# Layer 0 with fp32 sums beside the count table and 16 dense blocks, the last sweep's blocks in the sweeps' PSUM banks, and attention in four stages

## The chip, the core and the metric

The kernel runs on one core of a Trainium2 chip. Five engines work from queues of their own: PE (TensorE, the matrix multiplier), DVE (VectorE), ACT (ScalarE), POOL (GpSimd) and SP (SyncE). In this kernel POOL issues the indirect gathers, SP issues nearly all other loads and stores, and ACT a few. The metric is device time in microseconds. Before the change it is the median of three runs.

## What is computed

A graph of N = 12500 nodes and E = 200000 edges, sorted by target. Each node has D = 256 features. Three layers take the mean over the incoming edges; a residual and a layernorm follow; then one attention step with K = 4 heads of R = 16, a gradient step, and a second layernorm.

```python
def _sage_layer(x, src, dst, inv_deg, W_self, W_neigh, b):
    agg = jax.ops.segment_sum(x[src], dst, num_segments=N_NODES)
    mean = agg * inv_deg[:, None]
    return x @ W_self + mean @ W_neigh + b
h = relu(_sage_layer(x, ...W0)); h = relu(_sage_layer(h, ...W1)); h = _sage_layer(h, ...W2)
z = _layernorm(x + h)

ZU = jnp.einsum('nd,kdr->knr', z, U)
logits = (ZU[:, src] * ZU[:, dst]).sum(-1) / sqrt(R)
alpha = softmax of logits over the edges of each dst
agg = segment_sum(alpha[..., None] * ZU[:, src], dst)
Z_half = 0.5 * z + 0.5 * einsum('k,knr,kdr->nd', softmax(head_w), agg, U)
residual = Z_half - (Z_half @ Dmat.T) @ Dmat
out = _layernorm(z + relu(Z_half + 0.5 * (residual @ Dmat) - 0.05))
```

## The kernel before

The edges are cut into NG = 112 groups of 1792 edges (14 columns of 128), in the order of their targets. Two ways lead to the sums of a layer.

*Groups.* POOL gathers the source rows of a group with 14 indirect DMAs (L118) into a buffer xg. DVE builds a one-hot matrix oh of edge against node (L458). ACT rounds the rows to fp32r (hi, L799), and DVE takes the rest (lo, L801), so that two fast matmuls, one of hi and one of lo, give fp32 accuracy. In layer 0 these are two matmuls per column j (L808, L809), in layers 1 and 2 one of twice the width (L805). All columns of a group add into pA; a carry (L465) shifts in the sums of the group before. sage_post then transposes the node's own row and the mean through the PSUM bank pT (L344, L368) and multiplies both by the weights into the bank pO (L348, L371). In layer 2, sage_end makes a layernorm, and project (L379 to L389) makes the attention's inputs, again through pT. finish hands out the tiles to store.

*Dense blocks.* The last NDL[l] blocks of 128 nodes of a layer go another way. During layer 0, form() builds a table cnt_d of how often each source occurs for each target: DVE compares (L626), PE multiplies (L634, 1024 matmuls), ACT writes bytes (L637) into the window tile win. A sweep runs over all 98 blocks of source rows for 4 (layer 0) or 8 (layers 1 and 2) target blocks at once. Each step loads rows hz and counts c8, ACT widens the counts (L706), and PE does 4 or 8 matmuls (L712) into the banks px. The results go to aggT (L724), and end_block finishes each target block like a group (L344, L348, L685, L689, and project in layer 2). The blocks of one sweep are finished during the next sweep; those of the last sweep follow at the layer's end.

NDL is (20, 32, 32): layer 0 has 90 groups and 490 sweep steps; layers 1 and 2 have 76 groups and 392 steps each.

*The order.* A Python loop over the groups emits everything. After each group, due(l, g) says how many sweep steps must have been emitted, and built(g) how many pieces of the table; the table is spread over the groups up to GB = 84. The last sweep's blocks begin at group NGS - LAG - sg, one per group, so the sweeps are spread over the groups up to there (66 in layers 1 and 2). A scheduler then reorders each engine's instructions by priority, with waits for data and for buffers; after() ties two instructions to an order by hand, as with the gathers and with PE's sweep steps. Two xg buffers are made at the start and filled early with the first two groups; layers 1 and 2 use a third one, "more". The one pT and the one pO bank serve groups and blocks alike.

*Attention.* For each of 112 groups SP loads zn, zb and the edges' row numbers, POOL gathers 14 columns of zs (four buffers), DVE builds oh, ACT the transposed one-hot ohT (L892, L893). For each half of the group PE spreads the target rows over the edges into pD (L905); DVE and ACT multiply, sum, exponentiate and weight (L910 to L923). PE adds up into pA (L926), with a carry (L465) from the group before; attention_post divides, transposes (L402), multiplies by gu into pO (L406), adds (L408) and makes the layernorm, and the group is stored. All of a group is emitted before the next group.

Of the kernel before, what the change touches and what calls it, by code (L numbers as in the profile page):

```python
# [9 lines left out]
F32 = mybir.dt.float32  # L10
F32R = mybir.dt.float32r
# [11 lines left out]
P = 128  # L23
NB = 125
TE = 125
GT = 14
# [5 lines left out]
ND = 32  # L32
NDL = (20, 32, 32)
SG0, SG = 4, 8
# [5 lines left out]
CP = 4  # L40
LAG = 2
G0 = 2
SMAX = 240.0
# [4 lines left out]
def tile_gnn_resnorm(  # L48
# [341 lines left out]

    def attention_post(wk, ps, zz, acc, eps=1e-16, op=OP.add):

        n = zz.shape[0]
        den = wk.tile([n, K], F32, name="den")
        nc.vector.tensor_scalar(den, acc[:, KR:AW], eps, None, op0=op)
        nc.vector.reciprocal(den, den)
        ag = wk.tile([n, KR], F32, name="ag")
        nc.vector.tensor_mul(ag.rearrange("p (k r) -> p k r", r=R),  # L398
                             acc[:, :KR].rearrange("p (k r) -> p k r", r=R),
                             den.unsqueeze(2).to_broadcast([n, K, R]))  # L400
        pa = ps.tile([P, n], F32, name="pT")
        nc.tensor.transpose(pa[:KR], ag, ident[:n, :n])  # L402
        agT = wk.tile([KR, n], F32, name="agT")
        nc.scalar.activation(agT, pa[:KR], AF.Copy)
        pg = ps.tile([n, D], F32, name="pO")
        nc.tensor.matmul(pg, agT, gu, start=True, stop=True)  # L406
        g = wk.tile([n, D], F32, name="g")
        nc.vector.tensor_add(g, zz[:, D:], pg)  # L408
        nc.scalar.activation(g, g, AF.Relu, bias=shrink[:n])
        nc.vector.tensor_add(g, zz[:, :D], g)  # L410
        return g, layernorm(wk, g, g)

# [54 lines left out]
    def fast_sage():  # L467
        with ExitStack() as fx:
# [82 lines left out]
            def chained(first, last):  # L551
                if chain[0] is not None:
                    after(chain[0], first)
                chain[0] = last

            counted = [0]

# [49 lines left out]
            def form(pool, psum):  # L607
# [6 lines left out]
                for i, u in enumerate(parts):  # L614
# [3 lines left out]
                    for i0 in range(0, P, CP):  # L618
# [9 lines left out]
                        for c in range(CP):  # L628
                            d = (i0 + c) * NC % P
                            if d == 0:  # L630
                                win = pool.tile([P, NP], U8, name="win", bufs=2).rearrange(
                                    "p (b d) -> p b d", d=P)
# [11 lines left out]

            def finish(l, lk, hn, po):

# [7 lines left out]
                zu = lk.tile([P, KR], F32, name="zu")  # L654
                made = project(lk, ps, hn, zu)
                sq = lk.tile([P, KR], F32, name="sq")
# [3 lines left out]
                nc.vector.tensor_max(top, top, nrm)  # L660
                return [(zu, zu_d), (hn, z_d)], made

            def sweeps(l, dk, dps, lk):
# [8 lines left out]

                def end_block(k, d, aggT):
                    at = N0 + (k + d) * P
# [4 lines left out]
                    if l == L - 1:  # L679
                        xb = lk.tile([P, D], F32, name="xb")  # L680
                        nc.sync.dma_start(xb, x[rows, :])
                    _, _, po = sage_own(wk, ps, wts[l], hb, True)
                    pn = ps.tile([P, D], F32, name="pO")
                    for c in range(DC):
# [6 lines left out]
                    sage_end(lk, l, wts[l], pn, hn[:, :D], xb)  # L691
                    for t, to in finish(l, lk, hn, pn)[0]:
                        nc.sync.dma_start(to[rows, :], t)
# [32 lines left out]
                for block in left:  # L726
                    end_block(*block)
                    yield []
# [3 lines left out]
            BUILDS = 3 + NU * PER  # L732
            GA, G1, GB = 3, 7, 84

            def due(l, g):
                sg, ahead = (SG, 0) if l else (SG0, G1)
                n, end = NDL[l] // sg * NQ, cuts[NDL[l]].NGS - LAG - sg
                if g >= end:
                    return n + min(sg, g + 1 - end)
                return max(0, n * (g + 1 - ahead) // (end - ahead))  # L740

# [8 lines left out]
            for l in range(L):  # L750
# [6 lines left out]
                with ExitStack() as lx:  # L757
# [10 lines left out]
                    for g in range(cut.NGS):  # L768
# [5 lines left out]
                        load_rows([(hb, table), (xb, x)][:1 if xb is None else 2], *at)  # L774
                        oh = onehot(wk, nodes, srel, F32R)
                        ahead = l == 0 and g < G0
                        if ahead:
                            last = early[g][1]
                        k = turn % (G0 + 1 if l else G0)
                        turn += 1  # L780
                        if k < G0:
                            xg = early[k][0]
                        else:
                            xg = dk.tile([P, GT, XW], F32, name="more", bufs=1)
                        for j in range(0 if ahead else GT):
# [4 lines left out]
                        pa = ps.tile([P, 2 * D], F32, name="pA")  # L790

                        if l:
                            hl = dk.tile([P, GT, 2, D], F32R, name="hl", bufs=1)
                            hi, lo = hl[:, :, 0], hl[:, :, 1]
                        else:
                            hi, lo = (dk.tile([P, GT, XW], F32R, name=n, bufs=1) for n in ("hi", "lo"))
                        hf = hi.bitcast(F32)
                        for j in range(0, GT, 2):
                            nc.scalar.activation(hi[:, j:j + 2, :W], xg[:, j:j + 2, :W], AF.Copy)  # L799
                        for j in range(GT):  # L800
                            nc.vector.tensor_tensor(lo[:, j, :D], xg[:, j, :D], hf[:, j, :D], op=OP.subtract)  # L801
                        for j in range(GT):
                            stop = g == 0 and j == GT - 1
                            if l:
                                end = nc.tensor.matmul(pa, oh[:, j], hl[:, j].rearrange("p i d -> p (i d)"),  # L805
                                                       start=j == 0, stop=stop)
                            else:
                                nc.tensor.matmul(pa[:, :W], oh[:, j], hi[:, j, :W], start=j == 0, stop=False)  # L808
                                end = nc.tensor.matmul(pa[:, :D], oh[:, j], lo[:, j, :D], start=False, stop=stop)  # L809
                        if g:  # L810
# [60 lines left out]
    def fast_attention():  # L871
        loads[0] = None
        H = GT // 2
        with tc.tile_pool(name="att", bufs=2) as wk, \
                tc.tile_pool(name="att_c", bufs=1, space=PSUM) as cps, \
                tc.tile_pool(name="att_ps", bufs=1, space=PSUM) as ps:
            nodes = group_consts(cps)
            before = None
            for g in range(NG):
                zb = wk.tile([P, 2 * D], F32, name="zb", bufs=3)  # L880
                zn = wk.tile([P, KR], F32, name="zn", bufs=3)
# [5 lines left out]
                                  .to_broadcast([P, GT * P]))  # L887
                zs = wk.tile([P, GT, KR], F32, name="zs", bufs=4)
                for j in range(GT):
                    gather(zs[:, j], zu_d, srcI[:, g, j:j + 1])  # L890
                oh = onehot(wk, nodes, rel[:, g], F32R)
                nc.scalar.activation(ohT.rearrange("p j e -> p (j e)"), rT, AF.Abs, bias=npidx)  # L892
# [6 lines left out]

                w = wk.tile([P, GT, 2 * AW], F32R, name="w")  # L900
                for a in (0, H):

                    pd = ps.tile([P, (H + 1) * 2 * KR], F32, name="pD", bufs=2)
                    for j in range(H):
                        nc.tensor.matmul(pd[:, j * 2 * KR:(j + 1) * 2 * KR], ohT[:, a + j],  # L905
                                         z2.rearrange("p k i r -> p (k i r)"), start=True, stop=True)

# [14 lines left out]
                    nc.scalar.activation(w[:, a:a + H, :AW], wf, AF.Copy)  # L922
                    nc.vector.tensor_tensor(w[:, a:a + H, AW:], wf, w.bitcast(F32)[:, a:a + H, :AW], op=OP.subtract)  # L923
                pa = ps.tile([P, 2 * AW], F32, name="pA")
                for j in range(GT):
                    nc.tensor.matmul(pa, oh[:, j], w[:, j],  # L926
                                     start=j == 0, stop=g == 0 and j == GT - 1)
                if g:
                    carry(wk, pa[:, :AW], delta[:, g:g + 1], before)
                acc = wk.tile([P, AW], F32, name="acc")  # L930
                part = wk.tile([P, AW], F32, name="part")
                nc.scalar.activation(part, pa[:, AW:2 * AW], AF.Copy)
                nc.vector.tensor_add(acc, part, pa[:, :AW])
                before = acc
                o, made = attention_post(wk, ps, zb, acc, 1e-30, OP.max)
                store_rows([(o, out)], g, made)


# [100 lines left out]
    def general_attention():  # L1039
# [40 lines left out]
        with tc.tile_pool(name="go", bufs=1) as wk, tc.tile_pool(name="go_ps", bufs=1, space=PSUM) as ps:  # L1080
            with tc.For_i(0, NBLK, 1) as i:
                rows = ds(i * NB, NB)
                zb = wk.tile([NB, 2 * D], F32, name="zb")
                nc.sync.dma_start(zb, z_d[rows, :])
                ab = wk.tile([NB, AW], F32, name="ab")
                nc.sync.dma_start(ab, acc_d[rows, :])
                o, _ = attention_post(wk, ps, zb, ab)
                nc.sync.dma_start(out[rows, :], o)
# [42 lines left out]
```

## Time and profile before

| | |
|---|---|
| median of three runs | 9464.18 us (9428.15 to 9476.44) |
| the profiled execution | 9457.81 us, span 9455.6 us |
| PE busy in the span | 5646.7 us (60%), 23556 matmuls |
| DVE busy | 4240.9 us (45%) |
| ACT busy | 3917.2 us (41%) |
| POOL busy | 4898.6 us (52%), 4982 instructions |
| granted PE clock, mean | 0.73 |
| moved by DMA | 1392.21 MB, 147 GB/s |
| sweep matmuls L712 | 8232, 2511.0 us busy |
| gathers L118 in attention | 1568, 1503.9 us busy, 1375.3 us idle before them |

The span is counted from the first to the last instruction, and 2.2 us of the profiled execution lie outside it. The busy time of an engine is the sum of its instructions; the idle time before an instruction is put down to whatever it waited for last. "remote" means that the profile found no instruction that released it at that time.

### The profile page before, as it was taken

Reading aid. Unit: us, or ns where it says so; the run is one execution under the profiler, and the core shown is the slowest. Engines: PE = TensorE matmul, PEld = TensorE weight load, DVE = VectorE, ACT = ScalarE, POOL = GpSimd, SP = SyncE. Lnnn points to the kernel's source line nnn. Section 1 sums busy time; section 2 is a strip of 40 time slices with the busy share of each in tenths; the row PEclk is TensorE's granted clock in tenths of the full one; section 3 lists DMA queues with packets and bytes.
Section 4 is the critical chain, followed back from the end, with each engine's and each line's share of the span. In section 5 each row is a group of like instructions: output and inputs, shape, how many; then the busy total and the mean of one; then the engine's idle time right before and its main releaser. Section 6 shows DMA issues by size and latency. Waiting matters only on the chain. (4 is left out here: it accounts for less than half of the span.)

```text
span 9455.6 us, 88266 instructions
## 1 busy us (share of the span) xinstructions
PE 5646.7 (60%) x23556; PEld 4373.7 (46%) x23556; DVE 4240.9 (45%) x11180; ACT 3917.2 (41%) x7165; POOL 4898.6 (52%) x4982
## 2 busy tenths in 40 slices
PE   4666777676577777764778787775333333333333
PEld 2455555555455656553556565653223223332323
DVE  5756555555333333333334444444244444444444
ACT  3655555554344444432344444432233333333333
POOL 4565555555455555554454444443455555555554
PEclk7788888887788888887888888886555555555555
DMA  7665666665466565654555555542222222222222
GB/s 205 219 199 190 200 216 203 206 212 178 156 185 191 188 191 186 191 158 127 161 177 174 173 174 165 168 152 75 60 76 76 72 75 77 75 72 76 76 76 61
DMA packets 836883, 1392.21 MB, mean 147 GB/s; under 512 B 187554, under 2 KB 452282, under 8 KB 832271
## 3 DMA queue, kind: packets, MB, share of 16 engines
q1 hardware_dynamic: 590624, 834.82, 27.1%
q0 software_dynamic: 213312, 496.82, 18.6%
q10 hardware_dynamic: 32431, 54.80, 1.7%
q8 instruction: 189, 3.10, 0.1%
q14 instruction: 327, 2.68, 0.1%
HBM read 1175.63 MB, written 210.33 MB: 147 GB/s over the span
## 5 line engine op out<-in xcount | busy, mean ns | idle before, releaser
L712 PE MATMUL px<-c,hz 128*128 128x512 f32 x8232 | 2511.0, 444 | 53.3 <-issue 45.9
L118 POOL DMA_INDIRECT zs<-zu_d,srcI x1568 | 1503.9, 959 | 1375.3 <-DVE sh L464 700.2
L118 POOL DMA_INDIRECT xg<-h_d,srcI x1428 | 1384.2, 969 | 1167.5 <-issue 342.7
L712 PEld LDWEIGHTS px<-c,hz 128*128 128x128 f32 x8232 | 1643.3, 206 | 554.9 <-issue 225.1
L118 POOL DMA_INDIRECT xg<-in_x_dram,srcI x1232 | 1296.6, 1052 | 994.6 <-DVE lo L801 477.6
L706 ACT ACTIVATE c<-c 128x1024 fp32r<-128x1024 uint8 (+1 forms) x1274 | 1124.3, 897 | 1370.9 <-remote 502.9
L458 DVE TENSOR_TENSOR oh<-rel,gconst 128x1792 fp32r<-128x1792 f32 x354 | 712.1, 2012 | 1008.2 <-remote 591.9
L118 POOL DMA_INDIRECT more<-h_d,srcI x700 | 669.7, 957 | 930.3 <-issue 367.0
L348 PE MATMUL pO<-ws,hT 128*128 128x256 f32 x1304 | 459.8, 485 | 460.8 <-DVE hT L345 343.3
L637 ACT ACTIVATE win<-pc 128x392 uint8<-128x392 f32 x1024 | 477.0, 503 | 526.3 <-remote 275.0
L805 PE MATMUL pA<-hl,oh 128*128 128x512 f32 x2128 | 591.4, 421 | 65.3 <-issue 25.7
L402 PE MATMUL pT<-ident,ag 128*64 128x128 f32 x112 | 46.8, 418 | 907.2 <-DVE ag L398 886.9
L634 PE MATMUL pc<-ob,oa 128*128 128x392 bf16 x1024 | 350.3, 377 | 353.0 <-ACT win L637 187.0
L348 PEld LDWEIGHTS pO<-ws,hT 128*128 128x128 f32 x1304 | 288.4, 237 | 577.3 <-DVE hT L345 392.2
L371 PE MATMUL pO<-wn,hT 128*128 128x256 f32 x968 | 335.5, 481 | 365.5 <-DVE hT L369 279.4
L799 ACT ACTIVATE hl<-xg 128x512 fp32r<-128x512 f32 x714 | 406.0, 621 | 336.3 <-remote 173.4
L801 DVE TENSOR_TENSOR hl<-xg,hl 128x256 fp32r<-128x256 f32 x1428 | 518.7, 416 | 27.7 <-ACT hl L799 19.0
L406 PE MATMUL pO<-gu,agT 64*128 64x256 f32 x224 | 136.5, 711 | 622.3 <-issue 551.4
L805 PEld LDWEIGHTS pA<-hl,oh 128*128 128x128 f32 x2128 | 415.9, 197 | 175.9 <-issue 39.2
L926 PE MATMUL pA<-w,oh 128*128 128x136 f32 x1568 | 420.3, 427 | 123.4 <-DVE bn_rs L335 54.3
L801 DVE TENSOR_TENSOR lo<-xg,hi 128x256 fp32r<-128x256 f32 x1260 | 454.7, 415 | 84.2 <-ACT hi L799 50.6
L408 DVE TENSOR_TENSOR g<-zb,pO 128x256 f32<-128x256 f32 x112 | 47.1, 421 | 942.0 <-remote 727.5
(225 smaller groups left out, 9700.7 us busy)
## 6 DMA issues: line engine op xcount, KB each, us to landing
hz<-hs_d SPq DMA_DIRECT2D x637, 512.0 KB
c<-cnt_d SPq DMA_DIRECT2D x112, 896.0 KB
ohT<-rel_d SPq DMA_DIRECT2D x112, 896.0 KB
hs_d<-hs SPq DMA_DIRECT2D x218, 256.0 KB
cnt_d<-win ACTq DMA_DIRECT2D x32, 1568.0 KB
c<-cnt_d SPq DMA_DIRECT2D x70, 448.0 KB
zb<-z_d SPq DMA_DIRECT2D x112, 256.0 KB
h_d<-hn SPq DMA_DIRECT2D x218, 128.0 KB
```

The costliest lines, as they stand in the source:

```text
L118: return nc.gpsimd.indirect_dma_start(out=dst_ap, out_offset=None, in_=table, in_offset=bass.IndirectOffsetOnAxis(ap=idx, axis=0))
L348: nc.tensor.matmul(po, hT[:, 0, c], wts[0][:, c], start=c == 0, stop=alone and c == DC - 1)
L371: nc.tensor.matmul(po, hT[:, 1, c], wts[1][:, c], start=False, stop=c == DC - 1)
L458: nc.vector.tensor_tensor(oh, r.unsqueeze(2).to_broadcast([P, GT, P]), nodes.unsqueeze(1).to_broadcast([P, GT, P]), op=op)
L634: mm = nc.tensor.matmul(pc.rearrange("p b d -> p (b d)"), oa[:, c], ob[:, c], start=True, stop=True)
L637: nc.scalar.activation(win[:, :, d:d + NC], pc, AF.Copy)
L706: nc.scalar.activation(c32.rearrange("p (k d) -> p k d", d=P), c8[:, :, b % CB], AF.Copy)
L712: made.append(nc.tensor.matmul(px[f][i], hz[:, b % ZB, a:a + P].bitcast(F32R), c32[:, i * 512:(i + 1) * 512], start=b == 0 and part == 0, ...
L799: nc.scalar.activation(hi[:, j:j + 2, :W], xg[:, j:j + 2, :W], AF.Copy)
L801: nc.vector.tensor_tensor(lo[:, j, :D], xg[:, j, :D], hf[:, j, :D], op=OP.subtract)
L805: end = nc.tensor.matmul(pa, oh[:, j], hl[:, j].rearrange("p i d -> p (i d)"), start=j == 0, stop=stop)
L926: nc.tensor.matmul(pa, oh[:, j], w[:, j], start=j == 0, stop=g == 0 and j == GT - 1)
```

## The change

1. *Layer 0's blocks.* NDL[0] goes from 20 to 16: 94 groups, 392 sweep steps.
2. *Layer 0's sums.* Groups 0 to 62 (g <= GB) multiply the gathered rows xg by an fp32 one-hot, one fp32 matmul per column, without hi and lo. Later groups split as before, but hi and lo lie in the two win tiles, which the table no longer needs by then. GB goes from 84 to 62, so the table is built by then; due() spreads half of layer 0's steps up to GB and half after it.
3. *Buffers.* G0 goes from 2 to 3: three xg buffers from the start, in all layers, and "more" is gone.
4. *The last sweep's blocks.* They come two per group (`2 * (g + 1 - end)`), and LAG goes from 2 to 1, so the sweeps of layers 1 and 2 are spread over 71 groups. end_block and finish get an argument bank: these blocks use the px banks of the sweeps in place of pT and pO. Within a px pair i, `px0i` stands for pT and `px1i` for pO.
5. *Attention.* attention_post becomes three functions; a group is a generator with four stages. Per round the newest group's first stage is emitted, then the second stage of the group before, and so on. in_order ties PE's order: pD of the newest group, pA and carry of the one before, the transpose of the second before, pO of the third before. zs has six buffers instead of four, zb six instead of three, oh, w and acc three instead of two.

```diff
-NDL = (20, 32, 32)
+NDL = (16, 32, 32)
-LAG = 2
-G0 = 2
+LAG = 1
+G0 = 3
...
-    def attention_post(wk, ps, zz, acc, eps=1e-16, op=OP.add):
+    def attention_mean(wk, acc, eps, op):
...
+        return ag
+
+    def attention_turn(wk, ps, ag):
+        n = ag.shape[0]
         pa = ps.tile([P, n], F32, name="pT")
-        nc.tensor.transpose(pa[:KR], ag, ident[:n, :n])
+        turn = nc.tensor.transpose(pa[:KR], ag, ident[:n, :n])
         agT = wk.tile([KR, n], F32, name="agT")
         nc.scalar.activation(agT, pa[:KR], AF.Copy)
+        return agT, turn
+
+    def attention_end(wk, ps, zz, agT):
...
-        nc.tensor.matmul(pg, agT, gu, start=True, stop=True)
+        mm = nc.tensor.matmul(pg, agT, gu, start=True, stop=True)
...
-        return g, layernorm(wk, g, g)
+        return g, layernorm(wk, g, g), mm
...
+            WB = max(NP, GT * XW * 4)
...
-                                win = pool.tile([P, NP], U8, name="win", bufs=2).rearrange(
+                                win = pool.tile([P, WB], U8, name="win", bufs=2)[:, :NP].rearrange(
...
-            def finish(l, lk, hn, po):
+            def finish(l, lk, hn, po, bank=ps):
...
-                made = project(lk, ps, hn, zu)
+                made = project(lk, bank, hn, zu)
...
+            class Spare:
...
+                def tile(self, shape, dt, name):
+                    return self.pool.tile(shape, dt, name=f"px{('pT', 'pO').index(name)}{self.i}")
...
-                def end_block(k, d, aggT):
+                def end_block(k, d, aggT, bank=ps):
...
-                    _, _, po = sage_own(wk, ps, wts[l], hb, True)
-                    pn = ps.tile([P, D], F32, name="pO")
+                    _, _, po = sage_own(wk, bank, wts[l], hb, True)
+                    pn = bank.tile([P, D], F32, name="pO")
...
                 for block in left:
-                    end_block(*block)
+                    end_block(*block, Spare(dps, block[1] % (sc // 512)))
                     yield []
...
-            GA, G1, GB = 3, 7, 84
+            GA, G1, GB = 3, 7, 62
...
-                n, end = NDL[l] // sg * NQ, cuts[NDL[l]].NGS - LAG - sg
+                n, end = NDL[l] // sg * NQ, cuts[NDL[l]].NGS - LAG - sg // 2
                 if g >= end:
-                    return n + min(sg, g + 1 - end)
-                return max(0, n * (g + 1 - ahead) // (end - ahead))
+                    return n + min(sg, 2 * (g + 1 - end))
+                if l:
+                    return n * (g + 1) // end
+
+                return max(0, n * (g + 1 - G1) // (GB - G1) // 2 if g < GB else n - n * (end - g - 1) // (end - GB) // 2)
...
-                        oh = onehot(wk, nodes, srel, F32R)
+
+                        halved = l or g > GB
+                        oh = onehot(wk, nodes, srel, F32R if halved else F32)
...
-                        k = turn % (G0 + 1 if l else G0)
+                        xg = early[turn % G0][0]
...
-                            hi, lo = (dk.tile([P, GT, XW], F32R, name=n, bufs=1) for n in ("hi", "lo"))
+                        elif halved:
+                            hi, lo = (tk.tile([P, WB], U8, name="win", bufs=2).bitcast(F32R).rearrange(
+                                "p (j d) -> p j d", d=XW) for _ in range(2))
+                        if halved:
...
+                            first, stop = j == 0, g == 0 and j == GT - 1
...
+                            elif halved:
+                                nc.tensor.matmul(pa[:, :W], oh[:, j], hi[:, j, :W], start=first, stop=False)
+                                end = nc.tensor.matmul(pa[:, :D], oh[:, j], lo[:, j, :D], start=False, stop=stop)
                             else:
...
+                                end = nc.tensor.matmul(pa[:, :W], oh[:, j], xg[:, j, :W], start=first, stop=stop)
...
-            before = None
-            for g in range(NG):
-                zb = wk.tile([P, 2 * D], F32, name="zb", bufs=3)
+            order, sums = [None], [None]
+
+            def in_order(first, last):
+                if order[0] is not None:
+                    after(order[0], first)
+                order[0] = last
+
+            def group(g):
+
+                zb = wk.tile([P, 2 * D], F32, name="zb", bufs=6)
...
-                zs = wk.tile([P, GT, KR], F32, name="zs", bufs=4)
+                zs = wk.tile([P, GT, KR], F32, name="zs", bufs=6)
...
-                oh = onehot(wk, nodes, rel[:, g], F32R)
+                oh = onehot(wk, nodes, rel[:, g], F32R, bufs=3)
...
-                w = wk.tile([P, GT, 2 * AW], F32R, name="w")
+                w = wk.tile([P, GT, 2 * AW], F32R, name="w", bufs=3)
...
+                    in_order(mm[0], mm[-1])
...
+                yield
                 pa = ps.tile([P, 2 * AW], F32, name="pA")
...
+                    mm.append(carry(wk, pa[:, :AW], delta[:, g:g + 1], sums[0]))
+                in_order(mm[0], mm[-1])
...
-                before = acc
-                o, made = attention_post(wk, ps, zb, acc, 1e-30, OP.max)
+                sums[0] = acc
+                ag = attention_mean(wk, acc, 1e-30, OP.max)
+                yield
+                agT, mm = attention_turn(wk, ps, ag)
+                in_order(mm, mm)
+                yield
+                o, made, mm = attention_end(wk, ps, zb, agT)
+                in_order(mm, mm)
                 store_rows([(o, out)], g, made)
+
+
+            live = []
+            for g in range(NG + 3):
+                if g < NG:
+                    live.insert(0, group(g))
+                for s in list(live):
+                    if next(s, live) is live:
+                        live.remove(s)
```

## The prediction

> **What bounds the kernel now.** I read the busy time by stage first, then the timeline of one stretch of each stage, then the waits. The stages are cut where the gathers change table: 76 us is the first gather of layer 0's main loop, 2403 and 4381 the first of layers 1 and 2, 6705 the first of attention. Columns are microseconds and, in brackets, instructions.
>
> ```profile
> core 0: us, PE busy (x) PEld busy (x) DVE busy (x) ACT busy (x) POOL busy (x), PEclk, DMA share, GB/s
> 76.00:2403.00 2327.00, 1581.50 (x7533) 1169.87 (x7532) 1367.78 (x4419) 1228.88 (x2694) 1311.88 (x1248) 0.81 0.63 204
> 2403.00:4381.00 1978.00, 1402.83 (x5614) 1098.55 (x5614) 723.90 (x1730) 826.38 (x1340) 1024.88 (x1064) 0.84 0.57 178
> 4381.00:6705.00 2324.00, 1681.41 (x6663) 1281.38 (x6663) 933.37 (x2589) 852.02 (x1446) 1029.06 (x1064) 0.82 0.49 152
> 6705.00:9456.00 2751.00, 965.09 (x3694) 814.50 (x3694) 1185.40 (x2350) 1006.46 (x1678) 1503.93 (x1568) 0.50 0.26 74
> ```
>
> No engine is full in any stage. Attention is the emptiest: 2751/112 = 24.6 us a group, of which DVE works 10.6 and POOL's 14 gathers, 1.25 us from start to start, take 17.5. Its timeline shows why:
>
> ```profile
> 8008.50 1.68 ACT L893 ACTIVATE ohT<-ohT 128x1792 fp32r<-128x1792 f32 x1
> ...
> 8020.74 0.27 ACT L404 ACTIVATE agT<-pT 64x128 f32<-64x128 f32 x1 [10.56 <-remote]
> ...
> 8027.04 0.42 DVE L408 TENSOR_TENSOR g<-zb,pO 128x256 f32<-128x256 f32 x1 [15.82 <-remote]
> ...
> 8033.66 0.95 POOL L118 DMA_INDIRECT zs<-zu_d,srcI  x1 [0.31 <-issue]
> 8038.95 0.23 ACT L932 ACTIVATE part<-pA 128x68 f32<-128x68 f32 x1 [10.94 <-remote]
> ...
> 8048.14 0.95 POOL L118 DMA_INDIRECT zs<-zu_d,srcI  x1 [13.53 <-DVE sh L464]
> ```
>
> POOL gathers two groups in one burst of 28 (7999.5 to 8034.6, 35.1 us) and then waits 13.5 us for a free zs buffer: a cycle of 48.6 us for two groups, the same through the whole stage. About 10 us into the burst everything but POOL stands still: ACT waits 10.6 us for the transpose L402, which PE shows as started at 8009.7; later 10.9 us for the carry L465, shown as started at 8023.6. Between the two lie some 3 us more. So 22.6 of 48.6 us are standstill, ending 4 us after the last gather; 26.0 us are left for two groups. In all stages I see the same: bursts of up to 14 gathers cost little, longer ones halt PE. Summing all gaps over 1.5 us in which PE, ACT and DVE are idle together: 363 us in layer 0, 341 and 310 in layers 1 and 2, 1262 in attention.
>
> In layer 0 POOL waits for the splitting of the gathered rows; at the end of layer 2 one chain alternates between a group and a dense block:
>
> ```profile
> POOL xg L118 <- DVE lo L801: 477.6, 166, 36.6
> ...
> 6375.00:6513.00 138.00, 58.28 (x192) 40.24 (x190) 61.33 (x162) 35.56 (x78) 80.91 (x83) 0.70 0.34 98
> 6513.00:6705.00 192.00, 121.52 (x333) 77.74 (x333) 69.28 (x216) 26.90 (x72) 1.20 (x2) 0.57 0.12 38
> ...
> 6601.03 0.70 PE pT L344 x2
> ...
> 6604.78 2.09 PE pO L685 x4
> ...
> 6615.06 0.70 PE pT L344 x2
> ```
>
> The last three lines are from the chain of waits: a block (L685) takes 14.0 us from 6601.0, then a group starts at 6615.1, and so on. Both use the one pT and the one pO bank. The last sweep ends at 6375; 330 us follow with no sweep matmul.
>
> **What the Trainium skill says.** "Perfetto Trace Analysis", Tensor Engine Instruction: the shown end of a matmul is an estimate from its size. The trace agrees: L402's row is 0.41 us long, its reader starts 11 us later. So a wait called remote here is a wait for PE. "FP8 and Floating Point Precision", TensorE Precision Notes: true fp32 takes four passes through the array. The trace shows it as two matmul rows of double length: start to start 0.216 us for 256 columns at full clock (L348), against 0.120 for a hi or lo matmul; 0.427 against 0.213 at half clock. "TensorE: Matmul & The Clock Gate", Part 1: an idle PE runs at half clock. It is 0.50 throughout attention, and a matmul of 128 columns follows the last one after 0.213 us. "PSUM — Partial Sum Buffer", The four PSUM rules: one matmul's output lies in one bank, so two blocks in the two pairs of px banks can be open at once; no row of before shows that.
>
> **The change, part by part.** The sum is made against the profiled execution, 9457.8 us, with a span of 9455.6; the median of three is 9464.2, 6 us more.
>
> *Layer 0, matmuls.* Groups 0 to 62 multiply fp32 rows directly: 63 x 28 rows, each dearer by 0.096 us at full clock (62% of the stage) or 0.213 at half: 1764 x 0.14 = +248 us of PE. 98 fewer sweep steps of 4 matmuls at 0.230 or 0.427 us: 392 x 0.305 = -120. Four more gathered groups at some 9 us of PE each, four fewer blocks at some 4.5: +36 - 18. PE: +146 us, all of which I put on the path, because PE is the fullest engine there.
>
> *Layer 0, ACT and DVE.* 59 groups fewer are split: 59 x 14 x 0.415 = -343 us of DVE, 59 x 7 x 0.639 = -264 of ACT; 98 conversions at 0.64 us go too. This was off the path by itself, but it held the xg buffers (the 478 us above) and stood in DVE's and ACT's order ahead of the table's work. Now PE's last matmul frees xg, and there are three. The table is built in 55 groups instead of 77, 16.3 matmuls a group instead of 11.6: +2.7 us of DVE, covered by the 5.8 us of lo gone. The four groups add 70 us to POOL, hidden while POOL has idle time (some 750 us). In 2327 us PE has 1486 of matmuls by start times and 363 of standstill; of the 478 us left I take a third off, -160; the bounds are 0 (other waits take their place) and -350. With a tail of two block slots instead of four, -45: layer 0 -60, between +140 and -250.
>
> *Layers 1 and 2, tail.* The sweeps are spread over 71 groups instead of 66, at 5.5 steps a group instead of 5.9, and the eight last blocks come two per group in banks of their own. Before, in layer 2, 330 us follow the sweeps. After: the main part gets five more groups, about 11 us each at its filling (7.4 us of PE at full clock): +55. Then four slots with a group and two blocks abreast. A chain is 14 us; PE has 8 to 17 us for three of them between full and half clock, DVE 5.8 + 2.0 + 3 x 3.7 = 19. I take 22, so 88, then 14 for the last group and 15 for its stores: 172, so -158. If the three chains still follow one another it is +0; perfectly abreast -200. Layer 1 has no projection and gathers up to its end; its tail is 4190 to 4381, 191 us. By the same count +40, then five slots of POOL's 17.5 and 30 to the next layer's first gather: 157, so -35 (+30 to -80). The third buffer "more" is the third xg buffer now: nothing.
>
> *Attention.* No instruction goes or comes. PE's order is fixed: pD of the newest group, pA and carry of the one before, the transpose of the second, pO of the third, so each step's input is a round old. Before, L406 stood in PE's queue right behind the L402 it needs, with ACT between, and DVE's L408 ahead of the next group's work. POOL's part is the same; zs has six buffers instead of four, zb six, w and oh three. On SP a store of group g-3 now stands beside the loads of g; its wait for the layernorm is over by then. The value: the 26.0 us of running per two groups can shrink to DVE's 2 x 10.6 = 21.2, -4.8; standstill stays 22.6, as the gathers set it. 56 x 4.8 = -269 us. Bounds: best, bursts end to end, 35.1 + 3.6 after the last gather = 38.7 a pair, -554; worst in the fourth case below.
>
> *Sum:* -60 - 35 - 158 - 269 = -522, so 8936 us in the profiled execution, 8940 by the median.
>
> **Rivals.**
> - *The scheduler had staged attention already.* Before, PE's rows do run groups g and g-2 in turn, and DVE is busy 21 of 26 running us. Against: L408 waits 942 us in all. Then attention gives -50, the rest as above: 9160.
> - *Standstill shrinks as well.* PE has other work when the transpose hangs, DVE can do one-hot and layernorm in it. Attention -554, layer 0 -150: 8560. Against: in the standstill PE itself hardly retires anything.
> - *Longer bursts, slower.* With six zs slots and three xg buffers POOL finds a free slot during the standstill, and a burst becomes 42 gathers or more. Burst 52.5 us; after its first 12 us it is standstill with, as now, a third of a group done per 26 us. Three groups then need 2.5 x 13 us of running, 12 of them in the burst: 20.5 + 52.5 + 4 = 77 us, 25.7 a group, +1.1 x 112 = +125. Layer 0 gets PE's +146 and a standstill of 25% instead of 16% (+200), the tails -193 - 45: 9457.8 + 233 = 9690. It decides from bursts of 42 on with PE not better fed. For it: the first burst of attention is 84 long and three quarters standstill. Against: layers 1 and 2 have three buffers and bursts of 14 to 19.
>
> **How the numbers follow.** Forecast 0.50, staged already 0.20, standstill shrinks 0.16, longer bursts 0.11, no visible change 0.03. The time is the first's, 8940. The range 8650 to 9300 leaves out most of the fourth and half of the third, some 0.2. Anything within 0.5% counts as the same, which is what a measurement of this kernel can tell. Faster 0.86, same 0.03, slower 0.11. The first three cases share the tail of layer 2, so they share the sign; by itself, the forecast lies between 8800 and 9080.
>
> **What would show it.** Attention's cycle near 44 us for 28 gathers, with L408 no longer waiting 942 us. In layer 0 two matmul rows per j at 0.216 us from xg, POOL's waits for lo gone for 63 groups. No more than 180 us from the last px matmul of layer 2 to attention's first gather. Wrong if gathers come in bursts of 42, if PE's standstill in layer 0 grows beyond 363 us, or if blocks still alternate with groups at 14 us each.

## The result, and the profile after

| | before | after |
|---|---|---|
| median | 9466.95 us (9428.15 to 9476.44, 4 runs) | 8993.96 us (8969.65 to 9022.81, 4 runs) |
| ratio | | 0.9509, 95% interval [0.9468, 0.955] |
| profiled span | 9455.6 us | 9006.1 us |
| layer 0 (to layer 1's first gather) | 2403 us, standstill 396 | 2467 us, standstill 345 |
| layer 1 | 1978, standstill 341 | 1892, standstill 237 |
| layer 2 | 2323, standstill 310 | 2150, standstill 266 |
| attention | 2747, standstill 1262 | 2493, standstill 956 |

Standstill is the sum of all gaps over 1.5 us in which PE, DVE and ACT are idle together, as in the prediction; layer 0 is counted here from the span's start, and attention to the last computing instruction, 4 us before the span's end. The stages differ by +64, -86, -173 and -254 us, -449 in all.

The busy time by stage of the changed kernel (microseconds, in brackets instructions):

```profile
core 0: us, PE busy (x) PEld busy (x) DVE busy (x) ACT busy (x) POOL busy (x), PEclk, DMA share, GB/s
41.00:2467.00 2426.00, 1696.06 (x7315) 1238.92 (x7313) 1136.51 (x3662) 1002.08 (x2192) 1282.31 (x1304) 0.80 0.58 187
2467.00:4359.50 1892.50, 1418.54 (x5614) 1114.68 (x5614) 722.15 (x1730) 824.31 (x1340) 1037.36 (x1064) 0.86 0.60 186
4359.50:6509.60 2150.10, 1626.45 (x6663) 1261.35 (x6663) 926.10 (x2587) 846.03 (x1446) 1036.13 (x1064) 0.85 0.53 164
6509.60:9006.10 2496.50, 909.74 (x3694) 790.98 (x3694) 1182.73 (x2352) 994.52 (x1674) 1508.55 (x1568) 0.50 0.28 81
```

In attention and in layers 1 and 2, DVE and ACT are busy for as long as before, to about 1%; the work is the same and lies closer together. In layer 0 DVE and ACT have over 200 us less to do, yet the stage is longer.

**Attention.** Two stretches of the timeline show the gain: first the end of a burst of 28 gathers and the next burst in the changed kernel.

```profile
8059.13 0.95 POOL L118 DMA_INDIRECT zs<-zu_d,srcI  x1 [0.30 <-issue]
8064.59 0.23 ACT L963 ACTIVATE part<-pA 128x68 f32<-128x68 f32 x1 [14.42 <-remote]
...
8067.88 0.61 DVE L950 TENSOR_TENSOR wf<-zs,pD 128x448 f32<-128x448 f32 x1
...
8068.76 1.02 POOL L118 DMA_INDIRECT zs<-zu_d,srcI  x1 [8.69 <-DVE acc L965]
...
8102.62 0.94 POOL L118 DMA_INDIRECT zs<-zu_d,srcI  x1 [0.31 <-issue]
...
8111.48 0.94 POOL L118 DMA_INDIRECT zs<-zu_d,srcI  x1 [7.92 <-DVE acc L965]
```

The standstill ends at 8064.6 (L963 had waited 14.4 us). 3.3 us later DVE reads the last of a zs buffer (L950), and at 8068.8 POOL goes on, 4.2 us after the standstill. In the kernel before the standstill ended at 8038.95 and POOL went on at 8048.14, 9.2 us later. The timeline of the kernel before shows what lay between:

```profile
8039.75 0.61 DVE L919 TENSOR_TENSOR wf<-zs,pD 128x448 f32<-128x448 f32 x1
...
8045.17 1.28 ACT L916 ACT_TABLE_LOAD   x1
8046.47 0.23 ACT L916 ACTIVATE wf<-lg 128x28 f32<-128x28 f32 x1
...
8047.27 0.60 DVE L919 TENSOR_TENSOR wf<-zs,pD 128x448 f32<-128x448 f32 x1
```

There only the first half of the group had come to L919; the second half still needed its exponential (L916), which stood behind a table load and the older group's work. (The profile names L464 and L965 as what POOL waited for. Neither touches zs, and at the end of each of these three pauses POOL starts 0.27 us after the end of an L919 or L950.) So the two cycles are 35.1 us of gathers, about 4 us to the end of the standstill, and 9.2 or 4.2 us to the next gather: 48.6 and 43 to 44 us. These stretches are typical: over the whole stage the median time from the last gather of a burst to the end of the standstill is 4.3 us in both kernels, and from there to the next gather 9.2 us before (53 bursts) and 4.1 after (48 bursts of 28). The whole stage divided by 56 pairs gives 44.5. The step that waited 942 us in all before (L408) waits 430 us now (L417).

**Layer 0.** In the page's costliest groups, the gathers of layer 0 stand, in the changed kernel, as

```profile
L118 POOL DMA_INDIRECT xg<-in_x_dram,srcI x1274 | 1249.8, 981 | 1027.2 <-PE pA L832 353.7
...
L832 PE MATMUL pA<-xg,oh 128*128 128x258 f32 x1764 | 477.1, 407 | 19.2 <-DVE oh L467 9.3
```

and in the kernel before as

```profile
L118 POOL DMA_INDIRECT xg<-in_x_dram,srcI x1232 | 1296.6, 1052 | 994.6 <-DVE lo L801 477.6
```

The number after the second bar is POOL's idle time before the gathers: 994.6/1232 and 1027.2/1274 are both 0.81 us a gather, 0.30 of it the usual pause between two gathers. The wait has mostly changed its name only, from the splitting (lo) to the matmuls that now read xg (L832). The time to the last sweep matmul is 2290/90 = 25.4 us a group before and 2424/94 = 25.8 after.

**The tail of layer 2.** The window from the last sweep matmul to attention's first gather, then the chain of waits inside it:

```profile
6408.70:6509.60 100.90, 76.81 (x355) 59.74 (x353) 69.45 (x230) 35.25 (x91) 16.07 (x17) 0.91 0.30 93
```

```profile
6444.04 0.66 PE px L384 x4
...
6445.83 0.86 PE px L348 x4
6446.70 0.11 PE px L344
6446.81 1.05 PE pO L371 x4
6447.86 0.86 PE px L704 x4
```

Within 5 us PE projects one block (L384), multiplies for another (L348, L704) and for a group (L371), in banks named px and pO. The clock granted is 0.91, where it was 0.57 to 0.70 before, and 334 us have become 101.

### The profile page after: what moved, and what is told of

Read it like the earlier page. It is cut to its first block, busy times and chain, and to the rows that moved or that the text cites. A ratio compares the mean times of both kernels' runs of the same rounds, so it can differ in the third digit from the quotient of the medians.

```text
span 9006.1 us, 86755 instructions
## 1 busy us (share of the span) xinstructions
PE 5653.6 (63%) x23292; PEld 4408.1 (49%) x23292; DVE 3972.1 (44%) x10371; ACT 3666.9 (41%) x6652; POOL 4894.2 (54%) x5038
## 3 DMA queue, kind: packets, MB, share of 16 engines
q1 hardware_dynamic: 569904, 802.70, 27.4%
q0 software_dynamic: 216000, 504.16, 19.9%
## 5 line engine op out<-in xcount | busy, mean ns | idle before, releaser
L118 POOL DMA_INDIRECT xg<-h_d,srcI x2128 | 2073.5, 974 | 1954.9 <-ACT mean L366 695.3
L118 POOL DMA_INDIRECT xg<-in_x_dram,srcI x1274 | 1249.8, 981 | 1027.2 <-PE pA L832 353.7
L467 DVE TENSOR_TENSOR oh<-rel,gconst 128x1792 fp32r<-128x1792 f32 (+1 forms) x358 | 721.4, 2015 | 1324.8 <-remote 934.5
L934 PE MATMUL pD<-z,ohT 128*128 128x128 f32 x1568 | 363.5, 418 | 1344.3 <-DVE wf L950 748.9
L934 PEld LDWEIGHTS pD<-z,ohT 128*128 128x128 f32 x1568 | 343.6, 330 | 1421.1 <-issue 969.7
L348 PE MATMUL pO<-ws,hT 128*128 128x256 f32 x1224 | 459.0, 510 | 598.9 <-DVE hT L345 509.6
L822 DVE TENSOR_TENSOR hl<-xg,hl 128x256 fp32r<-128x256 f32 x2128 | 773.7, 417 | 27.0 <-ACT hl L820 19.5
L820 ACT ACTIVATE hl<-xg 128x512 fp32r<-128x512 f32 x1064 | 604.3, 620 | 412.1 <-remote 185.7
L348 PEld LDWEIGHTS pO<-ws,hT 128*128 128x128 f32 x1224 | 284.2, 248 | 741.1 <-DVE hT L345 572.3
L826 PEld LDWEIGHTS pA<-hl,oh 128*128 128x128 f32 x2128 | 428.5, 203 | 124.8 <-issue 21.2
L832 PE MATMUL pA<-xg,oh 128*128 128x258 f32 x1764 | 477.1, 407 | 19.2 <-DVE oh L467 9.3
L941 DVE TENSOR_TENSOR zz<-zs,pD 128x896 f32<-128x896 f32 x224 | 241.3, 1078 | 548.8 <-remote 400.6
L957 PEld LDWEIGHTS pA<-w,oh 128*128 128x128 f32 x1568 | 348.4, 332 | 207.4 <-DVE zz L941 84.8
L832 PEld LDWEIGHTS pA<-xg,oh 128*128 128x128 f32 x1764 | 355.9, 206 | 135.8 <-issue 59.4
```

The lines of the kernel that those rows point to most:

```text
L118: return nc.gpsimd.indirect_dma_start(out=dst_ap, out_offset=None, in_=table, in_offset=bass.IndirectOffsetOnAxis(ap=idx, axis=0))
L348: nc.tensor.matmul(po, hT[:, 0, c], wts[0][:, c], start=c == 0, stop=alone and c == DC - 1)
L467: nc.vector.tensor_tensor(oh, r.unsqueeze(2).to_broadcast([P, GT, P]), nodes.unsqueeze(1).to_broadcast([P, GT, P]), op=op)
L832: end = nc.tensor.matmul(pa[:, :W], oh[:, j], xg[:, j, :W], start=first, stop=stop)
L934: mm = [nc.tensor.matmul(pd[:, j * 2 * KR:(j + 1) * 2 * KR], ohT[:, a + j], z2.rearrange("p k i r -> p (k i r)"), start=True, stop=True) f ...
L957: mm = [nc.tensor.matmul(pa, oh[:, j], w[:, j], start=j == 0, stop=g == 0 and j == GT - 1) for j in range(GT)]
```

## The experiments

The runs came in four lots, counting that of the result, each on a chip of its own. The chips were not alike: two show the large standstill and two hardly do, as the time of the kernel before tells (9467 and 9652 us, against 6920 and 6927). The changed kernel (after, after_again) and l0_ndl20 were run four times each, the other variants once. Stage times in microseconds, from the one trace of each:

| run | before, same chip | layer 0 | layer 1 | layer 2 | attention | whole |
|---|---|---|---|---|---|---|
| before | 9467 | 2403 | 1978 | 2323 | 2747 | 9458 |
| after | 9467 | 2467 | 1892 | 2150 | 2493 | 9008 |
| att_zs4 | 9652 | 2540 | 1932 | 2223 | 2508 | 9208 |
| att_unstaged | 9652 | 2506 | 1942 | 2251 | 2765 | 9470 |
| att_linear | 9652 | 2515 | 1933 | 2245 | 1221 | 7921 |
| tail_ps | 9652 | 2523 | 1940 | 2345 | 2526 | 9339 |
| l0_split | 6920 | 2000 | 1387 | 1490 | 2008 | 6890 |
| l0_two | 6920 | 1897 | 1388 | 1485 | 2000 | 6774 |
| half_px | 6920 | 1865 | 1384 | 1462 | 1998 | 6715 |
| att_zs3 | 6920 | 1881 | 1389 | 1487 | 2005 | 6768 |
| before_again | 6927 | 1874 | 1389 | 1640 | 2008 | 6917 |
| after_again | 6927 | 1884 | 1386 | 1488 | 2000 | 6760 |
| split_zs3 | 6927 | 2015 | 1383 | 1488 | 2001 | 6892 |
| l0_ndl20 | 6927 | 1826 | 1385 | 1490 | 1998 | 6703 |

A stage whose code is that of the changed kernel repeats within 34 us on the second chip (9652 us before; layer 0, 2506 to 2540) and within some 10 us on the last two; differences below these are read as none.

**The order or the buffers (attention).** The two halves of the attention edit, each alone.

```diff
-                zs = wk.tile([P, GT, KR], F32, name="zs", bufs=6)
+                zs = wk.tile([P, GT, KR], F32, name="zs", bufs=4)
```

> The changed kernel with four zs buffers instead of six, the staged order kept. Attention takes 2747 us before and 2493 us after. Theory 1 (the order: what runs after a standstill leads sooner to a free zs slot): attention stays at 2480 to 2560 us, whole kernel about 9000. Theory 2 (the two extra zs buffers let POOL run on): attention returns to 2680 to 2750 us, whole kernel about 9230.

```diff
             def in_order(first, last):
-                if order[0] is not None:
-                    after(order[0], first)
-                order[0] = last
+                pass
...
-            live = []
-            for g in range(NG + 3):
-                if g < NG:
-                    live.insert(0, group(g))
-                for s in list(live):
-                    if next(s, live) is live:
-                        live.remove(s)
-            assert not live
+            for g in range(NG):
+                for _ in group(g):
+                    pass
```

> The changed kernel with all its buffers, but attention emitted group by group again and PE's order left to the scheduler. Theory 1 (the order): attention returns to 2680 to 2750 us, kernel about 9230. Theory 2 (the buffers): attention stays at 2480 to 2560 us, kernel about 9000.

Four buffers with the staged order give 2508 us; all buffers without the order give 2765. The unchanged attention of that chip is in tail_ps, 2526 us. POOL's waits for a zs slot, from POOL's list of waits (sum, times, longest), first of the staged order with four buffers, then of the unstaged one, where L948 is the step that is L950 elsewhere:

```profile
POOL zs L118 <- DVE acc L965: 302.8, 39, 11.3
POOL zs L118 <- DVE wf L950: 140.9, 23, 12.7
```

```profile
POOL zs L118 <- DVE wf L948: 697.0, 49, 18.6
```

Without the order (the stages and PE's fixed sequence, taken away together) the whole gain is gone, and the two extra zs buffers give nothing that shows. The other added buffers (zb, oh, w, acc) were not taken away, so whether the order needs them is open. The rival that the scheduler had staged attention already falls with it.

**What the gathers cost (attention).**

```diff
-                for j in range(GT):
-                    gather(zs[:, j], zu_d, srcI[:, g, j:j + 1])
+                at = g % 6 * GE
+                nc.sync.dma_start(zs, zu_d[at:at + GE, :].rearrange("(p j) r -> p j r", j=GT))
```

> The changed kernel, with attention's 14 gathers of a group replaced by one plain load of as many rows in order, on SP's queue (it leaves out the selection of rows by the edges' sources; DVE, ACT and PE do the same work). Theory 1 (long bursts of gathers cause the standstill): idle stretches of PE, DVE and ACT together fall from 958 us to under 200, and attention takes 11 to 14 us a group, 1250 to 1550 us. Rival (the standstill is a wait in the chain between PE, ACT and DVE, whatever POOL does): attention stays above 2000 us.

```profile
6692.90:7914.10 1221.20, 902.05 (x3694) 788.78 (x3694) 1170.08 (x2351) 988.24 (x1674) 0.00 (x0) 0.50 0.49 166
```

This is attention's window, columns as above. The standstill is gone, not one gap over 1.5 us, and DVE is busy 1170 of 1221 us. With the indirect gathers gone the same work takes half the time (1221 against 2526 us); what remains is mostly DVE's 10.4 us a group. The run takes all gathers away, so it shows that they cause the standstill, and not that the length of their bursts does.

**The banks (tails).**

```diff
-                    end_block(*block, Spare(dps, block[1] % (sc // 512)))
+                    end_block(*block)
```

> The changed kernel with the last sweep's blocks in the pT and pO banks again, still two per group. After the last sweep matmul of layer 2 there are 334 us before and 101 us after. Theory 1 (own banks let the chains run abreast): 8 blocks and 5 groups follow one another at 14 us, so 180 to 230 us in layer 2 and some 110 to 150 (instead of 83) in layer 1. Rival (two blocks per group and the later start are enough): layer 2 stays at 100 to 130, layer 1 at 80 to 95.

In layer 2, 206 us follow the last sweep matmul, against 101 to 103 in the three other runs on that chip; in layer 1, 101 against 83 to 86, less than expected. The window and the chain of waits of this run:

```profile
6602.50:6808.00 205.50, 124.69 (x353) 79.24 (x351) 76.37 (x227) 35.82 (x89) 18.27 (x19) 0.63 0.15 47
```

```profile
6676.05 0.70 PE pT L344 x2
...
6679.80 1.92 PE pO L704 x4
...
6689.91 0.70 PE pT L344 x2
```

A block takes 13.9 us again and the next starts after it; the clock falls back to 0.63. The Trainium skill, "Perfetto Trace Analysis", Matmuls (under Optimizing Tensor Performance), advises that independent groups of matmuls rotate through different PSUM banks, so that reading out one overlaps the matmuls of the next; here the trace agrees, with 206 against 101 us. So of the 233 us between 334 and 101, the banks are worth about 105. The other 130, by difference, come with two blocks per group and the later end of the sweeps; this part is not shown by a run of its own, and the 334 is from another chip.

**Layer 0.** On the chips of these runs the standstill was small, so they take layer 0 apart there only.

```diff
-G0 = 3
+G0 = 2
...
-                        halved = l or g > GB
+                        halved = True
...
-                        xg = early[turn % G0][0]
+                        k = turn % (G0 + 1 if l else G0)
+                        xg = early[k][0] if k < G0 else dk.tile([P, GT, XW], F32, name="more", bufs=1)
...
-                            hi, lo = (tk.tile([P, WB], U8, name="win", bufs=2).bitcast(F32R).rearrange(
-                                "p (j d) -> p j d", d=XW) for _ in range(2))
+                            hi, lo = (dk.tile([P, GT, XW], F32R, name=n, bufs=1) for n in ("hi", "lo"))
```

> The changed kernel with layer 0's sums as before: every group split into hi and lo in tiles of their own, two xg buffers in layer 0 (a third, 'more', in layers 1 and 2, as before). The 16 blocks, the table by group 62 and everything else as changed. Layer 0 takes 2403 us before, 2467 after. Theory 1 (PE's work sets layer 0, and fp32 costs its 248 us there with nothing got back): layer 0 gets shorter by 150 us or more. Theory 2 (the splitting and the two buffers cost as much as the fp32 matmuls): within 60 us of the changed kernel's on the same chip. Theory 3 (fp32 is a gain, and what makes layer 0 longer is elsewhere, in the gathered groups that replace blocks): longer by 80 us or more.

```diff
-                        xg = early[turn % G0][0]
+                        xg = early[turn % (G0 if l or g < G0 else 2)][0]
```

> The changed kernel with two of its three xg buffers used from group 3 of layer 0 on (layers 1 and 2 use all three). Theory 1 (the third buffer takes POOL's waits for a buffer off the path): layer 0 gets longer by 80 to 200 us. Rival (POOL's wait was hidden): within 30 us.

```diff
-                            for part in range(2):
+                            for part in range(1):
...
-                                        start=b == 0 and part == 0, stop=b == NQ - 1 and part == 1))
+                                        start=b == 0 and part == 0, stop=b == NQ - 1))
```

> The changed kernel with half the sweeps' matmuls (it leaves out the products of the counts with the lo part of the rows; loads, count conversions and all else stay). Theory 1 (PE's work sets layers 0 to 2): 784 matmuls fewer at 0.23 to 0.43 us are 180 to 330 us less in layer 0, 1568 fewer 360 to 500 us less in each of layers 1 and 2. Rival (gathers, DMA and the chain between engines set them, PE waits): less than 60 us in layer 0 and less than 150 in each of the others.

The unchanged layer 0 of that chip is in att_zs3, 1881 us. Splitting every group with two buffers costs +119 us, using two buffers with the fp32 sums +16; so the fp32 sums themselves gain about 104, and the third buffer little. Half of the sweeps' matmuls are worth 16, 5 and 25 us in the three layers, where PE's own account would have 180 to 500. So PE hardly sets the layers there. POOL does for most of the time: a gather is issued every 1.25 us, a group takes 17.5 us at best, and in layer 0 of after_again a group takes 17.9 to 18.2 from group 30 on. The first 30 groups take 22.8 us each, and in its layer 2 a group from 40 on takes 19.5 to 20.2, which half the matmuls bring to about 18.

```diff
-NDL = (16, 32, 32)
+NDL = (20, 32, 32)
```

> The changed kernel with 20 dense blocks in layer 0 instead of 16: 90 groups instead of 94, 98 sweep steps more. Theory 1 (a gathered group costs its full slot, 17.5 us or more, and a sweep step hides beside it): layer 0 shorter by 40 to 110 us, the kernel 0.5 to 1.2% faster than the changed one. Rival (PE's work counts: 392 matmuls at 0.305 us are 120, four groups give back 36): layer 0 longer by 40 to 90 us.

Layer 0 is 58 us shorter with 20 blocks than with 16 (1826 against 1884). Its last gather comes 71 us earlier, four slots of 17.9, although there are 98 sweep steps more beside the gathers; behind the last gather 14 us of this are lost again. The kernel has a ratio of 0.9676 [0.9658, 0.9695] to the kernel before, the changed kernel on the same chip 0.9759 [0.9743, 0.9776]. It beats both; 6702.54/6760.17 is 0.9915, and the four times of each do not overlap. It was not run on a chip with large standstill.

**Shorter bursts (attention), inconclusive.**

```diff
-                zs = wk.tile([P, GT, KR], F32, name="zs", bufs=6)
+                zs = wk.tile([P, GT, KR], F32, name="zs", bufs=3)
```

> The changed kernel with three zs buffers in attention. Theory 1 (a standstill needs a burst of more than about 14 gathers; with fewer free slots POOL is held to shorter bursts and PE keeps running): bursts of 14, standstill under 700 us, attention under 2400 us. Rival (slots are released in pairs by the standstill itself, whatever their number): bursts of 28 stay, and POOL starts later, attention 2520 to 2700 us.

The second run joined this edit to the layer 0 of l0_split:

> Two edits in separate stages. Layer 0: sums by hi and lo in all groups and two xg buffers, as before the change, with the 16 blocks and the table by group 62. Attention: three zs buffers. Layer 0, theory 1 (the fp32 sums with their buffers gain, the four added gathered groups cost): longer than in the changed kernel by 60 to 140 us. Theory 2 (PE's work counts in full): shorter by 100 us or more. Attention, where standstill is large: theory 1 (shorter bursts, less standstill) under 2400 us, rival (released in pairs, later start) 2520 to 2700.

Both met chips with little standstill: attention took 2005 and 2001 us, as with six buffers, and all 1568 gathers followed one another with no pause over 0.6 us. Three buffers made no shorter bursts there, and whether shorter bursts help where the standstill is large was not seen. Layer 0 of the second run repeats the cost of splitting, +130 us.

**Both kernels on such a chip.** Unedited:

> The kernel before, once more, for its stages on the chip of these runs. Where standstill is large (kernel near 9500 us): layer 0 near 2400 to 2480, attention near 2750. Where it is small (kernel near 6900 us): if POOL's gathers at 17.5 us a group set the stages there, attention is near 2000 us as in the changed kernel, layers 1 and 2 differ by their tails alone (some 60 and 120 us), and layer 0 lies within 60 us of the changed kernel's.

> The changed kernel, once more, on the same chip. Theory 1 (the gain of attention comes from standstill, those of the tails do not): with large standstill 0.95 of the kernel before; with small standstill the 254 us of attention are gone and the ratio is 0.97 to 0.985.

Attention, windows of the changed kernel and of the one before:

```profile
4758.20:6758.20 2000.00, 910.16 (x3694) 790.98 (x3694) 1179.55 (x2351) 986.80 (x1674) 1500.13 (x1568) 0.50 0.36 101
```

```profile
4903.00:6911.00 2008.00, 976.66 (x3694) 818.21 (x3694) 1186.37 (x2352) 1015.81 (x1678) 1513.10 (x1568) 0.50 0.36 101
```

112 groups at 17.5 us are 1960: POOL's gathers follow one another with no pause over 0.32 us in either kernel, and the order has nothing left to gain. The same page of the skill, What "DMA-bound" means, names this sign: an issuing engine whose track is solid with DMA issues. The trace agrees nearly, with 0.95 us of issue and 0.30 between two gathers. The common gaps over 1.5 us sum to 227 us before and 339 after, while the stage gets 8 us shorter. Of these, 216 and 329 us end when gathered rows land (L910, L941), so here such gaps are waits for POOL's row of gathers, and their sum is no cost of its own. On the chip of the result they are of another kind: 24 of the 956 us of the changed kernel end so, and some 850 are remote. Layer 1 gains 3 us, not the 60 expected, because it too is a row of gathers: its tail shrinks from 173 to 86 us, but its main part grows from 1216 to 1300, and 76 x 17.5 = 1330 of its 1386 us are gathers. Layer 2, whose tail has no gathers, keeps its gain: 1640 to 1488. Layer 0 is 10 us longer.

## Why the prediction was right, and where its parts were not

*The sum.* -522 us was forecast for the profiled execution, -450 came. The terms of layer 2 and of attention were near in size; of these two only layer 2's was right in its path. Layer 1 gained more than its bound of -80 allowed. Layer 0 has the wrong sign: it missed by 124 us, and layers 1 and 2 made up 66 of these. That the sum came so near is in part luck.

*Layer 2, -158 forecast, -173 measured.* The step holds in both its parts: 55 us more before the last sweep matmul (60 measured), and 330 to 117 after it (334 to 101). That the chains run abreast because of the banks is shown by taking the banks away.

*Layer 1, -35 forecast, -86 measured.* The main part was put at +40 and came to +24, the tail at 157 less 40, 117, and came to 83. The term was sized too small: its five slots were priced at POOL's 17.5 us a group, but the gathers were nearly through when the last sweep matmul came, with 30 us to the last of them.

*Attention, -269 forecast, -254 measured.* The size was right, the split not. The prediction kept the standstill at 22.6 us a pair and let the running time shrink from 26.0 to 21.2. Measured, the standstill went from 22.6 to 956/56 = 17.1, and the time outside it grew to 27.4. The burst of 35.1 us and the 4.3 us from its end to the end of the standstill are the same in both kernels, so how much of the burst is standstill does not set the cycle. What had to be priced was the stretch between the end of the standstill and the next gather, 9.2 us against 4.2. A total that lies near the forecast does not confirm the path by which it was reached. The rival that the standstill shrinks as well has its mechanism half confirmed; its time, 8560, was far off, since bursts still end in a wait.

*Layer 0, -60 forecast, +64 measured.* This is the step that failed. The tail was right in kind (-45 forecast, 113 to 43 us measured), and so was the price of an fp32 row (0.216 us forecast at full clock, 0.217 measured from start to start of L832). The prediction took PE for the engine that sets the stage, counted PE's +146 us in full, took 160 us of waits off, and hid four more gathered groups behind POOL's idle time. On the chip of the result the wait per gather stayed at 0.81 us and the time per group at 25.4 to 25.8 us, so four more groups were four more slots: about 100 us, less the 70 of the tail, and the rest from the higher time per group. That PE's load hardly counts, that the fp32 sums gain, and that the groups cost a slot each, was shown on the chips with little standstill; it was not taken apart on the others.

*The rival of longer bursts.* After the opening burst, which grew from 84 to 112, no burst of the changed kernel's attention is longer than 28, with six zs buffers or four. Its mechanism was not seen. It also read the opening burst of before as three quarters standstill, where the common gaps sum to 65 of 105 us.

*What the prediction did not ask.* Its standstill is not the kernel's alone, and long bursts need not stop PE: on the chip of after_again all 1568 gathers of attention came in one row, and no common gap of the other engines was longer than 6.0 us, against 33.2 on the chip of the result. There the change is worth 2.4%, not 4.9%, and attention's share of that is 8 us.

## What to carry to other kernels

Find the queue whose slot every round needs, here 14 gathers of 1.25 us and POOL's waits between them, and price added or removed rounds in its slots, not in the busy time of the engine that looks fullest. When a wait disappears, look at what is named in its place and divide by the number of instructions: 0.81 us a gather stayed 0.81. Look at whether chains share a PSUM bank: with one pT and one pO bank they ran one after the other here although PE was idle for 39% of that tail (125 of 206 us busy), and the sweeps' banks, free at the end of the stage, let them run abreast.

## What the runs showed of the hardware that was not expected

The same kernel took 8994 us on one chip and 6760 on another. The first lines of the page and the line of the gathers' queue, for the changed kernel on the first chip and then on the last:

```profile
PE 5653.6 (63%) x23292; PEld 4408.1 (49%) x23292; DVE 3972.1 (44%) x10371; ACT 3666.9 (41%) x6652; POOL 4894.2 (54%) x5038
...
q0 software_dynamic: 216000, 504.16, 19.9%
```

```profile
PE 5134.8 (76%) x23292; PEld 4095.4 (61%) x23292; DVE 3964.3 (59%) x10371; ACT 3666.5 (54%) x6652; POOL 4900.6 (72%) x5038
...
q0 software_dynamic: 216000, 504.16, 26.6%
```

DVE, ACT and POOL are busy for the same time to 0.2%, and so is the gathers' queue: 19.9% of 9006 us and 26.6% of 6762 are 1792 and 1799 us of each of the 16 DMA engines. So these engines' instructions and the gathers' packets are not slower on the first chip, and those of the loads' queue q1 only by 2% (2468 against 2421 us); the time lies between them. In attention the standstill is 956 us on one and 339, nearly all of it waits for rows, on the other, in layers 1 and 2 it is 503 and 26. On the second chip, plain loads in place of the gathers took attention from about 2500 to 1221 us and the standstill to nothing. So in attention on that chip the other engines stand still because of the indirect gathers, and two chips show far more of it than the other two. How the gathers stop the other engines, and what makes the difference between the chips, stays open.
